# Polynomial convolution and attention on one core: the last quadratic orbit moved onto spare rows by GpSimd transfers

## Chip, core and metric

The kernel runs on one core of one Trainium2 chip. The metric is the time of one execution on the device in microseconds (us); lower is better. Engines are called as the profile calls them: PE (matrix), PEld (its weight loads), DVE (vector), ACT (scalar), POOL (GpSimd) and SP (the queue that issues most transfers).

## What is computed

The input x holds 32 images of 64 channels, 56 x 56 pixels each (N = 3136 pixels). The channels form 8 groups of 8. Two layers follow each other.

```python
# layer 0: polynomial of the 8 channels of a group, per pixel
p2 = x[:, :, _I2] * x[:, :, _J2]                       # 36 products of two
p3 = x[:, :, _I3] * x[:, :, _J3] * x[:, :, _K3]        # 120 products of three
y  = inp + (W2 @ p2 + b2) * beta2 + (W3 @ p3 + b3) * beta3 * 0.1
# layer 1: attention over the 3136 pixels of an image
g = clip(bn(conv1x1(y)), 0, 6)
f = softmax(softmax(theta.T @ theta, axis=1), axis=2)  # theta: first 32 channels of y
out = bn(depthwise3x3(f @ g / h * w)) + y
```

## The kernel before

**Pairs and steps.** The 32 images are worked in 16 pairs. A pair has 49 steps (`IT = 2 * NQ + 1`): a step handles 128 query pixels of one image. In a step PE makes the scores in two halves (`scores`, tile ps), DVE copies each half out of PSUM into the tile e with a running minimum, ACT runs two exponentials over 128 x 3136 values (`first_softmax` and `second_softmax`), and PE multiplies the result of three steps earlier (`LAG = 3`) with g into the accumulators av and ax (`attend`). Into the step's free places go the work of other pairs: convolution steps of a finished pair on DVE (tile y from tt), the matmuls that make g, and the polynomial of the next pair.

**The polynomial.** Its pixels are cut into 13 chunks (`PCS`, 242 pixels, the last one 232). A chunk of a pair has four parts k (two images, two halves of the groups; `ks` is `ALL`); for the first pair's second image only two (`TWO`). A tile of 128 rows is filled by transfers: 32 rows (8 channels of 4 groups) times `NSLOT = 4` slots, interleaved, so that slot s is every fourth row from s. Slot s pairs each channel with the one s further in its group. GpSimd multiplies two such tiles into q (the quadratic orbits 0 to 3) and q with a third tile into p, four times ("0", "2", "4", "b" in `LOADS`; the cubic orbits). PE turns each product into outputs with a 128 x 32 weight from wq, accumulating in `ax[:, AUX:]`. That is five rounds for each k. The sixth round is the last quadratic orbit, channel times channel four further: 32 rows for each k, made in one multiplication for all k (tile p4, from the load xc) and used with its own weight w4. The function `poly` issues the matmuls, `products` the multiplications, `poly_out` the DVE instruction that adds the bias and x and writes y.

**Order.** Every engine runs its instructions in the order in which they are issued (`Pinned`). The order of the products is that of the generator `products`: it goes on in `advance`, called twice a step, as soon as its loads are issued and there is room (`ROOM`: 8 tiles of q, 20 of p). `feed` lists the loads of a chunk, `load_next` issues them on SP, with limits on buffers (`XB`: 7, 13 and 3) and a credit for each half-step. A buffer of a pool is given out again in the order in which it became free.

**Units.** `rounds` in the main loop cuts the six rounds of a chunk into three units of two; a unit stands in a step of its own, so that three units (called U0, U1 and U2 below) take three steps. After some chunks one to three units of g follow, so that the next chunk begins three or four steps after this one. Counted from the loop, the distances between the first units of the 13 chunks in a pair are 4, 4, 3, 4, 3, 3, 3, 4, 3, 3, 4 and 3 steps, and 8 steps from the last chunk to the next pair's first. `split` shares the blocks of `attend` between the two halves of a step by the weight of the units there.

**The start.** The first image is made ahead of the loop in seven slices (`first_loads`, `first_products`, `first_poly`), with DVE doing the products. During the first pair's 49 steps both the rest of pair 0 (13 chunks of two parts) and all of pair 1 (13 chunks of four) are made, so it holds half as much polynomial again as a later pair. The last pair has none.

`_poly_weights` gives each product its weight once: a product that came in an earlier orbit gets zero weight (`if m in seen: continue`). Slot 2's cubic orbit with "0" is channel, channel two further, channel; slot 0 has had it with "2". So the rows of slot 2 in round 1 carry weight zero.

Of the kernel before, what the change touches and what calls it, by code (L numbers as in the profile page):

```python
# [9 lines left out]
FP = mybir.dt.float32  # L10
AF = mybir.ActivationFunctionType
ALU = mybir.AluOpType
# [4 lines left out]
C = G * CPG  # L17
# [18 lines left out]
PCH = -(-N // NPC)  # L36
# [18 lines left out]
]  # L55
NSLOT = 4
NRND = 5
NPROD = sum(1 + len(bs) for _, bs in STEPS)


# [9 lines left out]
def tile_poly_conv_attention(  # L70
# [43 lines left out]
    pe, dve, act, pool, sync = map(Pinned, (nc.tensor, nc.vector, nc.scalar, nc.gpsimd, nc.sync))  # L114

    const = ctx.enter_context(tc.tile_pool(name="const", bufs=1))
    xp = ctx.enter_context(tc.tile_pool(name="xp", bufs=2))
    prp = ctx.enter_context(tc.tile_pool(name="prp", bufs=8))
# [9 lines left out]


    wq = const.tile([128, NRND, 2, 32], FP, name="wq")  # L130
    w4 = const.tile([128, 128], FP, name="w4")
    at = 0
    for s, (_, bs) in enumerate(STEPS):
        for h in range(2) if s < NSLOT else ():
            act.dma_start(
                out=wq[s::NSLOT, :, h, :],
                in_=wpoly[h * 32 : h * 32 + 32, at : at + NRND, h * 32 : h * 32 + 32],
            )
        if s == NSLOT:
            act.dma_start(out=w4, in_=wpoly[:, at, :])  # L140
        at += 1 + len(bs)
    colt = const.tile([128, len(COLS)], FP, name="colt")
    wdt = const.tile([128, 9], FP, name="wdt")
# [12 lines left out]
    for k in range(2):  # L156
        pe.matmul(
            out=ax[:, k * 256 : k * 256 + 256],
            lhsT=w4,
            rhs=wq.rearrange("p k h o -> p (k h o)")[:, :256],  # L160
            start=(k == 0),
            stop=True,
            skip_group_check=True,
        )
# [11 lines left out]
    def row(name):  # L176
        return rowt[:, ROWS.index(name), :]
# [32 lines left out]
    frs = {}  # L210
# [11 lines left out]
    def first_loads(c):  # L222
# [16 lines left out]
        for d in (0, 1):  # L239
# [3 lines left out]
            for k in (0, 1):  # L243
                load(t[k * 32 : k * 32 + 32, :], k, 4 * d, 0, 1)

    def first_products(c):
        xs = fxs[c]

        def product(a, b):
            p = fp[fat["p"] % len(fp)]  # L250
            fat["p"] += 1
            dve.tensor_tensor(p, a, b, ALU.mult)
            return p

        q = {k: product(xs["0", k], xs["a", k]) for k in (0, 1)}
        frs[c] = [q] + [{k: product(q[k], xs[a, k]) for k in (0, 1)} for a in "024b"]
        dve.tensor_tensor(xs["c", 1], xs["c", 0], xs["c", 1], ALU.mult)
        frs[c].append(dict.fromkeys((0, 1), xs["c", 1]))

    first_loads(0)  # L260
    first_loads(1)
# [4 lines left out]
    dve.tensor_scalar(b3row, row("beta3_0"), CONV3_SCALE, None, ALU.mult)  # L266
    for k in range(NRND):
        by = row("beta2_0") if k == 0 else b3row
        w = wq[:, k, :, :].rearrange("p h o -> p (h o)")
        dve.tensor_tensor(w, w, by, ALU.mult)  # L270
    for half in (0, C):
        w = w4[:, half : half + C]
        dve.tensor_tensor(w, w, row("beta2_0"), ALU.mult)
    bias0 = const.tile([128, 1], FP, name="bias0")
    dve.tensor_tensor(bias0, col("b3"), col("beta3_0"), ALU.mult)
    dve.tensor_scalar(bias0, bias0, CONV3_SCALE, None, ALU.mult)
# [80 lines left out]
    def prefetch():  # L357
        while plan and held[plan[0][0]] < XB[plan[0][0]] and credit[0] >= 1:
            load_next()


    ROOM = {"q": 8, "pr": 20}
    taken = dict.fromkeys(ROOM, 0)

    def products(n, c, ks):

        p0, w = PCS[c]  # L370
        ident = f"{n}_{c}_{ks[0]}"

        def use(name, k=None):
            key = n, c, ks, name, k
            return loaded.pop(key)

        x0 = {}
        rounds = [{}]
        both = []
        prods[n, c, ks] = rounds, both  # L380
        yield "q", len(ks)
        for k in ks:
            yield "load", (n, c, ks, "a", k)
            x0[k] = use("0", k)
            xa = use("a", k)
            q = prp.tile([128, PCH], FP, name=f"q_{ident}_{k}", tag="q", bufs=ROOM["q"])[:, :w]
            pool.tensor_tensor(q, x0[k], xa, ALU.mult)
            rounds[0][k] = q
            held["xs"] -= 1
            prefetch()  # L390
        for r, of in enumerate(("0", "2", "4", "b")):
            rounds.append({})
            yield "pr", len(ks)
            for k in ks:
                if of != "0":
                    yield "load", (n, c, ks, of, k)
                xr = x0[k] if of == "0" else use(of, k)
                p = prp.tile([128, PCH], FP, name=f"p_{ident}_{k}_{r}", tag="pr", bufs=ROOM["pr"])[:, :w]
                pool.tensor_tensor(p, rounds[0][k], xr, ALU.mult)
                rounds[-1][k] = p  # L400
                held["x0" if of == "0" else "xs"] -= 1
                prefetch()
        at = slice(ks[0] * 32, ks[-1] * 32 + 32)
        yield "load", (n, c, ks, "c", None)
        yield "pr", 1
        both += use("c")
        p4 = prp.tile([128, PCH], FP, name=f"p4_{ident}", tag="pr", bufs=ROOM["pr"])[at, :w]
        pool.tensor_tensor(p4, both[0], both[1], ALU.mult)
        rounds.append({k: p4 for k in ks})

    feeds = []

    def advance():
# [20 lines left out]
            feeds[0] = gen, None  # L434

    def feed(n, c, ks):
        todo = [("x0" if name == "0" else "xs", name, k) for k in ks for name in "0a"]
        for name in "24bc":
            todo += [("xc", name, None)] if name == "c" else [("xs", name, k) for k in ks]
        for tag, name, k in todo:  # L440
            plan.append((tag, (n, c, ks, name, k)))
        feeds.append((products(n, c, ks), None))
# [12 lines left out]
    def poly(n, c, ks, rs):  # L455

        p0, w = PCS[c]
        rounds = prods[n, c, ks][0]
        at = slice(ks[0] * 32, ks[-1] * 32 + 32)
        for r in rs:  # L460
            for k in ks:
                pe.matmul(
                    out=ax[k * 32 : k * 32 + 32, AUX : AUX + w],
                    lhsT=wq[:, r, k % 2, :] if r < NRND else w4[at, k * 32 : k * 32 + 32],
                    rhs=rounds[r][k],
                    start=False,
                    stop=(r == NRND),
                    skip_group_check=True,
                )
            taken["pr" if r else "q"] -= 1 if r == NRND else len(ks)  # L470

    def poly_out(n, c, ks):

# [276 lines left out]
    def unit(hs, what, todo, out_, blocks):  # L750
        units.append((hs, what, todo, out_))
        weight[hs] = weight.get(hs, 0) + blocks
        if out_ is not None:
            leaves.add(hs)
# [17 lines left out]
            put(hs // 2, f"aux{hs % 2}", go)  # L772

    def poly_unit(n, c, ks, rs, hs):
        ends = rs[-1] == NRND
        unit(
            hs,
            FOR_POLY,
            lambda: poly(n, c, ks, rs),
            (lambda: poly_out(n, c, ks)) if ends else None,  # L780
            1 + 3.6 * len(rs),
        )
        if ends and c == NPC - 1:
            for j in (0, 1):
                if 2 * j in ks:

                    t = hs // 2 + 1 if j == 0 or n == 0 else (n * IT) + 2
                    put(t, "loads", lambda j=j: load_theta(2 * n + j))
# [15 lines left out]

    def first_poly(c):
        p0, w = FCS[c]
        for r in range(NRND + 1):
            for k in (0, 1):
                pe.matmul(
                    out=banks[c][k * 32 : k * 32 + 32, :w],  # L810
                    lhsT=wq[:, r, k, :] if r < NRND else w4[:C, k * 32 : k * 32 + 32],
                    rhs=frs[c][r][k],
                    start=(r == 0),
                    stop=(r == NRND),
                    skip_group_check=True,
                )

# [40 lines left out]
    for n in range(NP):  # L858
# [2 lines left out]
        ga = [("g", n + 1, qs, 0) for qs in GS]  # L861

        def rounds(m, c, ks, per):
            return [("p", m, c, ks, list(range(r, r + per))) for r in range(0, NRND + 1, per)]

        todo = []
        if n == 0:
# [3 lines left out]
            for c in range(NPC):  # L871
                todo += rounds(1, c, ALL, 2)
                if c >= NPC // 2 + 1:
                    k = min(2 if c < NPC - 1 else len(ga), sum(ready(g[2]) <= c for g in ga))
# [3 lines left out]
            at = [2 * base + free[i * (len(free) - 1) // (len(todo) - 1)] for i in range(len(todo))]  # L878
        elif n + 1 == NP:
            todo = gb  # L880
            at = [2 * (base + LAG) + 3 + 4 * i for i in range(len(gb))]
        else:
            at = []
            h = 2
# [38 lines left out]
    for n in range(NP):  # L923
# [11 lines left out]
        for i in range(9 * NB):  # L935
            at = more[i * (len(more) - 1) // (9 * NB - 1)]
# [12 lines left out]
    while t < last + LAG or beside:  # L949
        u = t - LAG  # L950
        new, old = t < last, 0 <= u < last
        todo = []
        if old:
            n, kind, q = tile_at(u)
            todo = [2 * n, 2 * n + 1] if kind == 2 else [2 * n + kind]
# [7 lines left out]
        both = len(todo) == 2  # L963
# [31 lines left out]
def _poly_weights(w2, w3):  # L995
# [4 lines left out]
    at3 = {ijk: k for k, ijk in enumerate(t3)}  # L1000
    wts = np.zeros((2, 2, CPG, 4, NPROD, 2, 2, CPG, 4), np.float32)
    seen = set()
# [18 lines left out]
    assert len(seen) == len(at2) + len(at3)  # L1021
    return wts.reshape(128, NPROD, 128)

# [42 lines left out]
```

## Time and profile before

| | us |
|---|---|
| median of three runs | 4949.45 |
| lowest and highest | 4947.52 and 4963.6 |
| the profiled execution's own time | 4948.12 |
| its span, first to last instruction | 4946.3 |

| engine | busy us | share of the span |
|---|---|---|
| PE | 4734.2 | 96% |
| PEld | 3218.8 | 65% |
| DVE | 4125.5 | 83% |
| ACT | 4554.4 | 92% |
| POOL | 3222.6 | 65% |

The profile is one execution. A group line gives engine, operation, output and inputs, how often, then busy time and mean duration of one instruction, then the engine's idle time ahead of them and what ended it. In a timeline line stand start, duration, engine, operation, how many were merged, and in square brackets the idle time just before with what ended it. All lines are of the helper at line 108, so the names of the tiles tell the instructions apart. Matmuls of one unit run side by side in different columns of the array, so the busy time of a group is what counts and not number times mean.

### The profile page before, as it was taken

To read this page: it belongs to the slowest core of one execution; us is meant where nothing else is said; L and a number is where in the kernel's file an instruction comes from. 1 tells how busy PE (TensorE), PEld (TensorE's weight loads), DVE (VectorE), ACT (ScalarE), POOL (GpSimd) and SP (SyncE) were. 2 spreads that over 40 slices of the span, in tenths; PEclk is the share of its full clock that TensorE was granted. 3 is DMA by queue.
4 is the path that set the end of the run, shared out by engine and by line. 5 is a ranking of instruction groups with operands and counts; after the bars stand their busy time and mean duration, and the time that the engine had idled before them with its cause. 6 is when DMAs were issued, how large, how long until landed. Compare 5 with 4: busy or idle time off the path is not lost.

```text
span 4946.3 us, 264020 instructions
## 1 busy us (share of the span) xinstructions
PE 4734.2 (96%) x118122; PEld 3218.8 (65%) x118122; DVE 4125.5 (83%) x6100; ACT 4554.4 (92%) x2356; POOL 3222.6 (65%) x4335
## 2 busy tenths in 40 slices
PE   6898999999999999999999999999999999999887
PEld 2555666666666666666666666666666666666665
DVE  6545898888888898888889889898888889888887
ACT  1667999999999999999999999999999999999996
POOL 2677685858858586785857768585875858678000
PEclk8999999999999999999999999999999999999999
DMA  7555656565565655556555565656556565654201
GB/s 205 145 152 156 147 144 153 144 152 141 145 141 151 146 145 149 143 143 146 149 143 144 149 143 142 154 144 150 142 145 143 150 144 144 153 142 126 45 11 34
DMA packets 884318, 685.66 MB, mean 139 GB/s; under 512 B 290924, under 2 KB 869356, under 8 KB 879084
## 3 DMA queue, kind: packets, MB, share of 16 engines
q1 hardware_dynamic: 875180, 659.46, 52.5%
q8 instruction: 924, 15.14, 1.3%
q10 hardware_dynamic: 8000, 9.30, 0.6%
q14 instruction: 214, 1.75, 0.1%
HBM read 565.65 MB, written 25.69 MB: 120 GB/s over the span
## 4 chain that ended last, share of the span: by engine, by line
PE 77%; DVE 12%; DMA 3%; issue 3%; ACT 3%; POOL 1%; SPq 1%; ACTq 0%; DVEq 0%; POOLq 0%
PE av L108 33%; PE ps L108 26%; PE ax L108 18%; DVE e L108 10%; ACT e L108 3%; DMA xc_None<-in_x_dram 1%; POOL p L108 1%; DVE y L108 1%; DMA first<-in_x_dram 1%; DVE num L108 1%; DMA x<-in_x_dram 1%; SPq L108 1%; DMA xa<-in_x_dram 0%; DVE rd L108 0%; ACTq L108 0%
## 5 line engine op out<-in xcount | busy, mean ns | idle before, releaser
L108 PEld LDWEIGHTS av<-gq,e 128*64 128x64 f32 x64512 | 2012.2, 138 | 943.9 <-issue 936.2
L108 ACT ACTIVATE e<-e,nm 128x3136 f32<-128x3136 f32 x784 | 2283.6, 2913 | 279.9 <-DVE e L108 264.0
L108 POOL TENSOR_TENSOR p<-q,x 128x242 f32<-128x242 f32 (+1 forms) x2418 | 1824.3, 788 | 815.6 <-PE ax L108 801.2
L108 ACT ACTIVATE e<-e,rz 128x3136 f32<-128x3136 f32 x784 | 2270.3, 2896 | 0.0
L108 PE MATMUL av<-gq,e 128*64 128x65 f32 x64512 | 2225.5, 225 | 3.9 <-ACT e L108 3.1
L108 DVE TENSOR_SCALAR_CACHE_REDUCE e<-ps 128x1568 f32<-128x1568 f32 x784 | 1403.7, 1790 | 314.1 <-PE ps L108 294.2
L108 DVE TENSOR_SCALAR_CACHE_REDUCE e<-ps,nm 128x1568 f32<-128x1568 f32 x784 | 1448.6, 1848 | 255.7 <-PE ps L108 250.1
L108 PE MATMUL ps<-th 32*64 32x392 f32 x25088 | 1449.4, 515 | 120.7 <-DVE e L108 110.7
L108 POOL TENSOR_TENSOR q<-x,xa 128x242 f32<-128x242 f32 x806 | 574.2, 734 | 226.0 <-DMA xa<-in_x_dram 218.0
L108 DVE SCALAR_TENSOR_TENSOR y<-tt,wdt,y 128x605 f32<-128x605 f32 (+6 forms) x711 | 713.1, 1003 | 6.4 <-DMA tt<-tr 5.2
L108 POOL TENSOR_TENSOR p<-q,xb 128x242 f32<-128x242 f32 x806 | 573.9, 739 | 212.3 <-PE ax L108 204.5
L108 PEld LDWEIGHTS ps<-th 32*64 32x64 f32 x25088 | 369.8, 130 | 463.7 <-DVE e L108 381.5
L108 PE MATMUL ax<-gq,e 128*64 128x65 f32 x12288 | 489.7, 222 | 0.7 <-issue 0.6
L108 PE MATMUL ax<-p,wq 128*32 128x242 f32 (+1 forms) x6448 | 481.9, 374 | 1.8 <-POOL p L108 0.2
L108 PEld LDWEIGHTS ax<-gq,e 128*64 128x64 f32 x12288 | 425.0, 138 | 1.0 <-issue 1.0
L108 PEld LDWEIGHTS ax<-p,wq 128*32 128x32 f32 x6448 | 178.4, 109 | 111.8 <-POOL p L108 19.1
L108 POOL TENSOR_SCALAR y<-y,bias 128x616 f32<-128x616 f32 (+2 forms) x79 | 146.9, 1860 | 98.9 <-PE ax L108 98.9
L108 POOL TENSOR_TENSOR p<-xc_None 128x242 f32<-128x242 f32 (+3 forms) x208 | 127.6, 614 | 109.5 <-DMA xc_None<-in_x_dram 91.0
L108 DVE SCALAR_TENSOR_TENSOR y<-ax,bias,xc_None 128x242 f32<-128x242 f32 (+3 forms) x208 | 97.1, 467 | 116.8 <-PE ax L108 116.8
L108 PE MATMUL ax<-wit,y 128*64 128x64 f32 x3136 | 144.2, 223 | 11.7 <-issue 7.5
L108 PE MATMUL ax<-p,w 128*32 128x242 f32 (+1 forms) x1612 | 123.9, 370 | 32.1 <-POOL p L108 32.1
L108 ACT ACTIVATION_READ_ACCUMULATOR e<-e,nm 128x1 f32 x784 | 145.5, 186 | 0.0
(86 smaller groups left out, 1389.4 us busy)
## 6 DMA issues: line engine op xcount, KB each, us to landing
x<-in_x_dram SPq DMA_DIRECT2D x2232, 121.0 KB
xa<-in_x_dram SPq DMA_DIRECT2D x744, 121.0 KB
xb<-in_x_dram SPq DMA_DIRECT2D x1488, 60.5 KB
th<-y SPq DMA_DIRECT2D x124, 392.0 KB
xc_None<-in_x_dram SPq DMA_DIRECT2D x360, 121.0 KB
x<-in_x_dram SPq DMA_DIRECT2D x186, 116.0 KB
out_dram<-y SPq DMA_DIRECT2D x60, 308.0 KB
tt<-tr SPq DMA_DIRECT2D x128, 100.0 KB
```

The costliest lines, as they stand in the source:

```text
L108: i = f(*args, **kw)
```

## The change

The sixth round goes. The 32 rows of a k in p4 are now copied, by a transfer that GpSimd issues, onto the rows of slot 2 in that k's product of round 1, whose own values there are not needed; the weight of the last orbit is added into wq at those rows, where it was zero. So that p4 is there in time it is made first in a chunk, and its load is listed first; so that the transfer has time to land, round 1 is the last round that PE takes: the order of rounds is 0, 2, 3, 4, 1. A chunk of four k then has two units of two rounds and one of a single round (for two k: three rounds and two). The slices of the start do the same, with seven times two transfers.

```diff
+SPARE = (2, 1)
+ORDER = (0, 2, 3, 4, 1)
...
-    w4 = const.tile([128, 128], FP, name="w4")
+    w4 = const.tile([128, 2, 32], FP, name="w4")
+    dve.memset(w4, 0.0)
...
+    def scatter(p, p4):
+
+        pool.dma_start(out=p[SPARE[0] :: NSLOT, :], in_=p4)
...
-        frs[c].append(dict.fromkeys((0, 1), xs["c", 1]))
+        for k in (0, 1):
+            scatter(frs[c][SPARE[1]][k], xs["c", 1][k * 32 : k * 32 + 32, :])
...
+    wr = wq[:, SPARE[1], :, :].rearrange("p h o -> p (h o)")
+    dve.tensor_tensor(wr, wr, w, ALU.add)
...
         prods[n, c, ks] = rounds, both
+        at = slice(ks[0] * 32, ks[-1] * 32 + 32)
+        yield "load", (n, c, ks, "c", None)
+        yield "pr", 1
+        both += use("c")
+        p4 = prp.tile([128, PCH], FP, name=f"p4_{ident}", tag="pr", bufs=ROOM["pr"])[:, :w]
+        pool.tensor_tensor(p4[at, :], both[0], both[1], ALU.mult)
         yield "q", len(ks)
...
                 pool.tensor_tensor(p, rounds[0][k], xr, ALU.mult)
                 rounds[-1][k] = p
+                if r + 1 == SPARE[1]:
+                    scatter(p, p4[k * 32 : k * 32 + 32, :])
...
-        yield "load", (n, c, ks, "c", None)
-        yield "pr", 1
-        both += use("c")
-        p4 = prp.tile([128, PCH], FP, name=f"p4_{ident}", tag="pr", bufs=ROOM["pr"])[at, :w]
-        pool.tensor_tensor(p4, both[0], both[1], ALU.mult)
-        rounds.append({k: p4 for k in ks})
...
-        for name in "24bc":
-            todo += [("xc", name, None)] if name == "c" else [("xs", name, k) for k in ks]
+        todo = [("xc", "c", None)]
+        todo += [("x0" if name == "0" else "xs", name, k) for k in ks for name in "0a"]
+        for name in "24b":
+            todo += [("xs", name, k) for k in ks]
...
-                    lhsT=wq[:, r, k % 2, :] if r < NRND else w4[at, k * 32 : k * 32 + 32],
+                    lhsT=wq[:, r, k % 2, :],
                     rhs=rounds[r][k],
                     start=False,
-                    stop=(r == NRND),
+                    stop=(r == ORDER[-1]),
...
-            return [("p", m, c, ks, list(range(r, r + per))) for r in range(0, NRND + 1, per)]
+            return [("p", m, c, ks, ORDER[r : r + per]) for r in range(0, NRND, per)]
```

In all 806 transfers are issued in the loop, 26 for pair 0 and 52 for each of the 15 other pairs, each of 32 rows of 968 bytes.

## The prediction

> **What bounds the kernel now.** I read the busy table and the chain first, then the steady stretch by itself, since the 49 steps of pair 0 differ from the rest.
>
> ```profile
> PE 4734.2 (96%) x118122; PEld 3218.8 (65%) x118122; DVE 4125.5 (83%) x6100; ACT 4554.4 (92%) x2356; POOL 3222.6 (65%) x4335
> ...
> PE 77%; DVE 12%; DMA 3%; issue 3%; ACT 3%; POOL 1%; SPq 1%; ACTq 0%; DVEq 0%; POOLq 0%
> ...
> L108 PE MATMUL ax<-p,w 128*32 128x242 f32 (+1 forms) x1612 | 123.9, 370 | 32.1 <-POOL p L108 32.1
> ```
>
> They suggest that PE is the bound and that the removed round (`ax<-p,w`, 123.9 us busy and 32.1 us of waiting) is worth up to 156 us. The windows and the waits of 1500 to 3000 us say less:
>
> ```profile
> 1500.00:3000.00 1500.00, 1472.41 (x37747) 1015.38 (x37738) 1310.39 (x1911) 1453.96 (x753) 1069.94 (x1425) 1.00 0.57 146
> ...
> ACT e L108 <- DVE e L108: 40.3, 113, 2.1
> ...
> POOL p L108 <- PE ax L108: 376.8, 125, 28.4
> ```
>
> ACT issues three instructions a step, so 753 are 251 steps of 5.98 us, 293 us a pair. ACT is busy 5.79 us of each and waits 0.16 (40.3 / 251), 7.9 us a pair: that is all a faster PE can win. POOL, busy 71%, waits in that stretch mostly for PE to free its buffers, and no wait of PE for POOL is listed there: POOL is ahead. The timeline shows where ACT waits:
>
> ```profile
> 2031.36 2.92 ACT L108 ACTIVATE e<-e,nm 128x3136 f32<-128x3136 f32 x1
> 2031.42 0.91 PE L108 MATMUL ps<-th 32*64 32x392 f32 x16
> ...
> 2033.58 0.62 PE L108 MATMUL ax<-p,wq 128*32 128x242 f32 x8
> 2034.01 0.59 PE L108 MATMUL ax<-p,w 128*32 128x242 f32 x8
> ...
> 2037.45 2.91 ACT L108 ACTIVATE e<-e,nm 128x3136 f32<-128x3136 f32 x1 [0.29 <-DVE e L108]
> ...
> 2037.62 0.91 PE L108 MATMUL ps<-th 32*64 32x392 f32 x16
> ...
> 2043.42 2.91 ACT L108 ACTIVATE e<-e,nm 128x3136 f32<-128x3136 f32 x1 [0.17 <-DVE e L108]
> ```
>
> This step has U2 and a unit of g; PE needs 6.20 us for it (2031.42 to 2037.62). ACT's starts are 6.09 and 5.97 apart here, against 5.86 where ACT runs without a break. So only 0.23 + 0.11 us are lost around such a step.
>
> **Part 1: the removed round.** In the step shown it takes 0.43 us (2033.58 to 2034.01, one round's distance); PE's 6.20 become 5.77, under 5.86. In the timeline of this pair ten of the 13 chunks show this loss at their last unit, so 10 x 0.34 = 3.4 us a pair, 14 pairs (1 to 14): **-48 us**. In all other steps ACT covers the removal. Bounds: 0 to 7.9 x 14 = 110.
>
> **Part 2: POOL's added work.** POOL's 1069.94 us over 1500 are 16.1 us for each chunk (209 us a pair, 13 chunks, its bias additions `y<-y,bias` included). The change issues four transfers a chunk between the products of round 1. Each waits for its product (POOL's own semaphore), and only then are its descriptors made; the next product stands behind it. No transfer from POOL is in this trace. The nearest row is SP's, and it is of another kind of queue:
>
> ```profile
> 2106.95 0.56 SPq L108 DMA_DIRECT2D x<-in_x_dram  x1
> ...
> 290.86 1.16 SPq L108 DMA_DIRECT2D xc_None<-in_x_dram  x2
> ...
> 296.54 0.61 POOL L108 TENSOR_TENSOR p<-xc_None 128x242 f32<-128x242 f32 x1 [2.46 <-DMA xc_None<-in_x_dram]
> ```
>
> By that row an issue is 0.56 us. The Trainium skill, DMA: Bandwidth & Descriptors, section Specifications, gives about 0.6 us to the first byte for the hardware-made descriptors of SP, which the row agrees with, and about 1 us for GpSimd's, made in software by its own cores. I take 1.0, since the other half of that table fits here, plus 0.1 for the product's semaphore (estimate; bounds 0.65 to 1.6 together). Four make 4.4 us. By the row alone the sum below would have no waits of PE and end 48 us lower than before; by the page it ends above.
>
> A second wait comes with it. Buffers are given out in the order in which they became free. p4 is free after its fourth transfer; three products of round 2 take the three buffers free before it, so the fourth takes p4's own and must wait until all four transfers have landed. Behind it on POOL stand nine products of the chunk, and SP's next loads wait for the buffers that those free. Landing: the xc load above took 4.5 us from the end of its issue to its reader (292.02 to 296.54), for 121 KB from HBM twice over. The skill's same page (Anatomy of one DMA) has about 2.0 us fixed plus bytes / 436e3, an estimate of 2.1 us for 31 KB. Three products cover 2.1 us. So the wait is 0 by the rule and 2.4 by the row; I take **0.8**, as the copy is smaller and not from HBM, but shares DMA engines 57% busy. With 0 the waits of PE below would be 1 to 2 us a pair, with 2.4 some 25.
>
> Together 16.1 + 4.4 + 0.8 = **21.3 us a chunk**. With ACT's 5.86 us a step, a chunk that begins three steps after the last has 17.6 us, one of four steps 23.4. So POOL loses 3.7 in the short ones and regains 2.1 in the long ones. Its reserve: round 2 may not start before PE's U0 of the chunk before (its buffers), and is wanted at the next U0. Of 17.6 us, the unit (1.0), five products (3.8), one transfer and the wait (1.9) use 6.7; for U1 the unit and eight products use 7.2. So about 10.4 us of lateness cost nothing. The distances are 4, 4, 3, 4, 3, 3, 3, 4, 3, 3, 4, 3, 8 steps, and the 8 wipes all lateness out. Lateness: chunk 3 has 3.7, chunk 4 1.6, then 5.3, 9.0, 12.7 (PE waits 2.3, leaving 10.4), 8.3, 12.0 (1.6), 14.1 (3.7), 8.3, 12.0 (1.6). PE waits **9.2 us a pair**, 129 in 14. PE then has no reserve, since ACT is fed step by step. The point from which this decides: with an overrun under 2.7 us a short chunk (transfers plus wait 4.2 us together, 0.86 us a transfer at my 0.8) PE never waits; each 0.1 us above it costs about 1 us a pair.
>
> **Part 3: pair 0.** POOL has no lead there:
>
> ```profile
> 296.54 0.61 POOL L108 TENSOR_TENSOR p<-xc_None 128x242 f32<-128x242 f32 x1 [2.46 <-DMA xc_None<-in_x_dram]
> 297.11 2.03 POOL L108 TENSOR_TENSOR q<-x,xa 128x242 f32<-128x242 f32 x3
> 300.40 7.93 POOL L108 TENSOR_TENSOR p<-q,x 128x242 f32<-128x242 f32 x12
> ...
> 314.62 0.61 POOL L108 TENSOR_TENSOR p<-xc_None 128x242 f32<-128x242 f32 x1 [2.95 <-DMA xc_None<-in_x_dram]
> ```
>
> A chunk takes 18.1 us, of which 14.1 are products and the rest waits for loads that SP issues back to back (26 a chunk at about 0.6). The 5.2 us of transfers and waiting go first into those waits: 14.1 + 5.2 = 19.3 against about 18.5, 0.8 x 13 = 10; the two-part chunks likewise 7.4 + 2.6 = 10.0 against 9.6, 5. If nothing is absorbed it is 13 x 5.2 + 13 x 2.6 = 101. I take **+30**, nearer to the absorbed end.
>
> **Part 4, at nothing.** The seven slices of the start lose a round and wait for 14 transfers; their loads cover it (POOL's first product waits 81 us), at worst 5 us either way. The extra memset and additions on wq are a few DVE instructions. The xc load moves from the end of a chunk's list to its front: in SP's endless order (..., b, xc, 0, a, ...) it keeps its neighbours; it holds its buffer one chunk longer, and with three of them SP could wait a step for `poly_out`, hidden while POOL is ahead by a chunk's loads. The copies add 25 MB to 686. PE's round 1 waits for a transfer issued about a chunk earlier; the cover is gone only if POOL is late, which part 2 counts.
>
> **Sum.** -48 + 129 + 30 = +111 on the profiled execution's 4948.1: 5059; the median of the runs stands 1.3 above it: **5060 us**.
>
> **The rivals.** *POOL's transfers exceed its reserve* (the forecast, 0.67): for it speak 16.1 of 17.6 us already used in short chunks; against it, that no transfer of POOL is in the trace. It runs from 4965 to about 5270 (1.4 us a transfer: overrun 4.9, 22 us a pair, less 3.4, by 14, plus 60).
>
> *The transfers are cheap* (0.28, faster): if one costs POOL under about 0.85 us, as SP's row would have it (4 x 0.65 = 2.6, overrun 1.1), PE never waits for POOL, pair 0 absorbs it, and part 1 remains: 4948 - 48 + 0 to 10, about 4905; down to 4840 if all of ACT's waits went.
>
> *It cancels* (0.05, within 0.3%, which is about what a measurement of this kernel can tell from no change, 15 us): about 0.95 us a transfer, where 5 to 6 us a pair meet the 3.4 and pair 0.
>
> *The full 156 us come off* (under 0.02, inside the second): it would need PE to be the limit in every step; the 5.86 us steps with two whole rounds in them speak against it.
>
> **Numbers.** Faster 0.28, same 0.05, slower 0.67. The range, 4898 to 5270, leaves a tenth at each end.
>
> **What would show it.** Right: POOL busy or waiting on its own transfers for over 20 us a chunk; waits of PE for POOL's p, or for its transfers, in 1500 to 3000 us, at chunks 7 to 12 of each pair; few waits of POOL for PE there; the fourth product of round 2 waiting for a DMA; pair 0 longer. Wrong: ACT's steps at 5.86 without exception and POOL still waiting for PE in each chunk; or a transfer of under 0.8 us between two products.

## The result, and the profile after

| | before | after |
|---|---|---|
| median, us | 4949.88 | 5223.52 |
| lowest and highest | 4947.52 to 4963.6 | 5204.94 to 5239.82 |
| span of the profiled execution | 4946.3 | 5203.2 |

The change made the kernel slower by 5.4%: ratio 1.0543, 95% interval 1.0518 to 1.0568. The forecast was 5060 us: 5223.5 lies inside its range, but the 274 us lost are two and a half times the 111 forecast. The reasons were not those of the forecast, as the trace of after shows. One execution of the 128-partition kernel below (5315.65 us) was in a slower state and is left out of that kernel's median and ratio; with it the median is the 5264 us that a later expectation names.

The page of after: the busy table, the chain by engine, and four groups (busy time, mean ns of one, then the idle time of the engine ahead of them and what ended it).

```profile
PE 4727.0 (91%) x116482; PEld 3195.6 (61%) x116482; DVE 4371.1 (84%) x6101; ACT 4553.9 (88%) x2356; POOL 3575.6 (69%) x5155
...
PE 51%; DVE 25%; issue 10%; DMA 5%; POOL 4%; ACT 2%; SPq 2%; ACTq 0%; POOLq 0%; DVEq 0%
...
L112 ACT ACTIVATE e<-e,nm 128x3136 f32<-128x3136 f32 x784 | 2283.1, 2912 | 529.6 <-DVE e L112 509.0
...
L112 DVE SCALAR_TENSOR_TENSOR y<-tt,wdt,y 128x605 f32<-128x605 f32 (+6 forms) x711 | 980.2, 1379 | 6.4 <-DMA tt<-tr 5.3
...
L112 POOL DMA_DIRECT2D p<-p x806 | 450.8, 559 | 252.9 <-POOL p L112 221.0
```

The same two groups of before, from its page:

```profile
L108 ACT ACTIVATE e<-e,nm 128x3136 f32<-128x3136 f32 x784 | 2283.6, 2913 | 279.9 <-DVE e L108 264.0
...
L108 DVE SCALAR_TENSOR_TENSOR y<-tt,wdt,y 128x605 f32<-128x605 f32 (+6 forms) x711 | 713.1, 1003 | 6.4 <-DMA tt<-tr 5.2
```

PE's share of the chain fell from 77% to 51%, DVE's rose from 12% to 25%. ACT's wait for DVE's e grew by 245 us (264.0 to 509.0). And one group that the change does not touch, the depthwise taps `y<-tt,wdt,y` on DVE (one of the nine products of the 3x3 convolution, added to y; two inputs, tt and y, are in SBUF), took 267 us longer for the same 711 instructions (713.1 to 980.2). POOL's transfer took 0.56 us, and its wait for the product ahead of it 0.3 us (252.9 us over 806).

The steady stretch of 1500 to 3000 us (the line of the windows first, its last three numbers being the granted clock, the DMA share and GB/s; then the waits):

```profile
1500.00:3000.00 1500.00, 1387.27 (x35082) 951.99 (x35082) 1326.09 (x1802) 1368.76 (x709) 1116.15 (x1602) 0.98 0.56 143
...
POOL p L112 <- PE ax L112: 191.7, 37, 28.5
...
ACT e L112 <- DVE e L112: 123.9, 73, 10.3
PE ps L112 <- DVE e L112: 106.4, 104, 9.4
POOL p L112 <- POOL p L112: 70.9, 243, 0.3
POOL p L112 <- DMA p<-p: 37.8, 27, 3.7
```

ACT's 709 instructions are 236 steps where before had 251. Its waits for DVE came to 40.3 us in 113 waits of at most 2.1; now they are 123.9 in 73, the longest 10.3. No wait of PE for POOL is among them. So something stops DVE for some ten microseconds at a time. The view of one tile gives the shortest, middle and longest duration in ns; before and after:

```profile
L108 DVE SCALAR_TENSOR_TENSOR y<-tt,wdt,y x711: 619/953/1471, 554.3 to 4940.8; 128x605 f32<-128x605 f32 x91, 128x616 f32<-128x616 f32 x45, 128x660 f32<-128x660 f32 x14, 128x672 f32<-128x672 f32 x8
```

```profile
L112 DVE SCALAR_TENSOR_TENSOR y<-tt,wdt,y x711: 619/998/12349, 568.0 to 5197.4; 128x605 f32<-128x605 f32 x91, 128x616 f32<-128x616 f32 x45, 128x660 f32<-128x660 f32 x14, 128x672 f32<-128x672 f32 x8
```

The middle hardly moves (953 to 998), but the longest is 12.35 us where it was 1.47. Over 3 us there are 26, before none. One of them in the timeline of after:

```profile
2615.01 0.56 POOL L112 DMA_DIRECT2D p<-p  x1 [0.29 <-POOL p L112]
...
2615.59 5.15 POOL L112 TENSOR_TENSOR p<-q,x 128x232 f32<-128x232 f32 x8
...
2617.14 10.70 DVE L112 SCALAR_TENSOR_TENSOR y<-tt,wdt,y 128x672 f32<-128x672 f32 x1
...
2623.82 2.65 POOL L112 TENSOR_TENSOR q<-x,xa 128x242 f32<-128x242 f32 x4
...
2627.41 0.56 POOL L112 DMA_DIRECT2D p<-p  x1 [0.29 <-POOL p L112]
...
2629.60 1.61 PE L112 MATMUL ps<-th 32*64 32x392 f32 x16 [9.39 <-DVE e L112]
...
2633.21 2.91 ACT L112 ACTIVATE e<-e,nm 128x3136 f32<-128x3136 f32 x1 [10.23 <-DVE e L112]
```

After a chunk's last transfer POOL runs product on product without a gap. A tap starts on DVE at 2617.14 and ends at 2627.84, just after POOL has paused for 0.29 us for its own product (ahead of 2627.41). DVE is in order, so the copies of e stand behind the tap: PE waits 9.39 us for e, ACT 10.23. I call this a hold.

Of the 26 taps over 3 us, 16 end like this one, 0.64 to 0.72 us after POOL's run has stopped for a wait. The other ten end with POOL still busy, each 1.41 us after POOL has begun its bias addition, which has one tensor input where a product has two:

```profile
1525.88 4.92 DVE L112 SCALAR_TENSOR_TENSOR y<-tt,wdt,y 128x605 f32<-128x605 f32 x1
...
1529.40 1.82 POOL L112 TENSOR_SCALAR y<-y,bias 128x616 f32<-128x616 f32 x1
...
1531.20 2.00 POOL L112 TENSOR_TENSOR p<-q,xb 128x242 f32<-128x242 f32 x3
```

In before, taps that start in a gap-free run last 1.08 us on average, against 0.82 when POOL is idle. Its gap-free runs reach 34.7 us, longer than any of after, and none holds a tap. So a long run by itself does not make a hold.

A hold has a second price. PE stands still behind it, and from 2624.7 to 2634.9 the clock granted to PE was half (the third number from the end in the first three lines); the first scores after the hold take 1.61 us (2629.60 above), where later ones take 0.92:

```profile
2614.00:2624.00 10.00, 6.06 (x156) 4.17 (x156) 10.00 (x5) 8.25 (x4) 9.67 (x16) 1.00 0.55 159
2624.70:2634.90 10.20, 5.30 (x88) 3.97 (x94) 7.52 (x8) 1.69 (x1) 5.51 (x9) 0.50 0.56 151
2635.00:2650.00 15.00, 14.18 (x364) 9.63 (x364) 14.20 (x17) 12.37 (x7) 10.91 (x14) 1.00 0.42 111
...
2637.74 0.92 PE L112 MATMUL ps<-th 32*64 32x392 f32 x16
```

From 550 to 5000 us after has 22 stretches at half clock, 154 us in all; 20 of them begin during a hold or within 3 us of its end. Before, from 550 to 4750 us, has none.

Where the time went, from the first e<-e,nm of each pair: 13 us in the start (97.1 to 110.1 us), 1 in pair 0, 241 in pairs 1 to 14 (17 a pair), 2 in pair 15. That is the 257 by which the spans differ.

### The profile page after: what moved, and what is told of

It is laid out like the page before. It is cut to its first block, busy times and chain, and to the rows that moved or that the text cites. A ratio compares the mean times of both kernels' runs of the same rounds, so it can differ in the third digit from the quotient of the medians.

```text
span 5203.2 us, 261265 instructions
## 1 busy us (share of the span) xinstructions
PE 4727.0 (91%) x116482; PEld 3195.6 (61%) x116482; DVE 4371.1 (84%) x6101; ACT 4553.9 (88%) x2356; POOL 3575.6 (69%) x5155
## 4 chain that ended last, share of the span: by engine, by line
PE 51%; DVE 25%; issue 10%; DMA 5%; POOL 4%; ACT 2%; SPq 2%; ACTq 0%; POOLq 0%; DVEq 0%
PE av L112 20%; PE ps L112 20%; DVE e L112 19%; PE ax L112 11%; DVE y L112 5%; POOL p L112 3%; ACT e L112 2%; SPq L112 2%; DMA th<-y 1%; DMA x<-in_x_dram 1%; DMA first<-in_x_dram 1%; POOL q L112 1%; DVE num L112 1%; DMA xa<-in_x_dram 1%; DMA xb<-in_x_dram 1%
## 5 line engine op out<-in xcount | busy, mean ns | idle before, releaser
L112 ACT ACTIVATE e<-e,nm 128x3136 f32<-128x3136 f32 x784 | 2283.1, 2912 | 529.6 <-DVE e L112 509.0
L112 POOL TENSOR_TENSOR p<-q,x 128x242 f32<-128x242 f32 (+1 forms) x2418 | 1728.3, 738 | 661.7 <-PE ax L112 441.1
L112 DVE SCALAR_TENSOR_TENSOR y<-tt,wdt,y 128x605 f32<-128x605 f32 (+6 forms) x711 | 980.2, 1379 | 6.4 <-DMA tt<-tr 5.3
L112 POOL DMA_DIRECT2D p<-p x806 | 450.8, 559 | 252.9 <-POOL p L112 221.0
L112 POOL TENSOR_TENSOR q<-x,xa 128x242 f32<-128x242 f32 x806 | 561.9, 727 | 45.7 <-DMA xa<-in_x_dram 36.5
L112 PE MATMUL ax<-p,wq 128*32 128x242 f32 (+1 forms) x6448 | 508.2, 377 | 34.2 <-POOL p L112 31.4
```

Of the source, the lines that this page charges most:

```text
L112: i = f(*args, **kw)
```

## The experiments

Three theories stood against each other. **1:** gap-free runs of POOL's products behind a transfer hold off DVE's two-input tap until POOL next pauses. **2:** POOL is late for PE (the forecast). **3:** the new order of products and buffers. A *pause* below is two small instructions on POOL, the second of which reads what the first wrote, so that POOL waits on its own semaphore. The last column of the table has the summed time of the taps in the profiled execution and how many lasted over 3 us. In the expectations "round 2" for the transfers' round is the one with index 1.

| kernel | median us | ratio to before, 95% interval | y<-tt,wdt,y us, over 3 us |
|---|---|---|---|
| after | 5223.5 | 1.0543 [1.0518, 1.0568] | 980.2, 26 |
| transfers on SP | 5428.3 | 1.0957 [1.0924, 1.0989] | 852.8, 29 |
| a pause after the transfers | 5003.5 | 1.0104 [1.0077, 1.0130] | 783.6, 10 |
| same instructions, no pause | 5269.2 | 1.0630 [1.0582, 1.0679] | 988.1, 30 |
| before + transfers | 5722.6 | 1.1582 [1.1513, 1.1651] | 1299.0, 98 |
| two pauses | 4989.6 | 1.0082 [1.0069, 1.0095] | 762.4, 3 |
| two pauses, early start | 4981.4 | 1.0059 [1.0048, 1.0071] | 760.4, 2 |
| before, no taps | 4947.6 | 0.9995 [0.9987, 1.0003] | left out |
| after, no taps | 4921.4 | 0.9939 [0.9925, 0.9954] | left out |
| grouped, two pauses, early start | 4921.0 | 0.9946 [0.9933, 0.9960] | 688.6, 0 |
| grouped, no pauses, early start | 5303.4 | 1.0703 [1.0670, 1.0737] | 1015.2, 59 |
| before + 32-partition products | 5597.5 | 1.1303 [1.1270, 1.1337] | 1202.2, 55 |
| before + 128-partition products | 5258.9 | 1.0595 [1.0559, 1.0632] | 966.2, 32 |
| the last with two pauses | 4972.3 | 1.0046 [1.0029, 1.0063] | 751.3, 2 |
| the 32-partition one with two pauses | 4994.1 | 1.0087 [1.0067, 1.0107] | 769.6, 0 |

Before itself: 4949 to 4951 us in these comparisons, taps 713.1 us, none over 3 us.

**Transfers on SP.**

```diff
-                    scatter(p, p4[k * 32 : k * 32 + 32, :])
+                    sync.dma_start(out=p[SPARE[0] :: NSLOT, :], in_=p4[k * 32 : k * 32 + 32, :])
```

> In the loop SP issues the 806 transfers, at the same places, instead of POOL; the start keeps POOL's. Theory 1 (after a transfer of its own POOL keeps the read path[...] through its whole run of products, and DVE's y<-tt, with two inputs in SBUF, stands behind it): y<-tt falls from a mean of 1.38 us back to about 1.0, none over 2 us, and the time goes to 4900 to 4960 us (the 48 us of the removed round won, the 13 us of the start still lost, some loads late on SP). Theory 2 (POOL's added time makes it late for PE): about the same time, since POOL is relieved of the transfers too, but y<-tt keeps its long ones. Theory 3 (the new order of p4, round 1 and the buffers is what costs): no change from 5224.

A miss: 5428 us, slower than after. The waits of the whole run show another cost:

```profile
POOL p L112 <- DMA p<-p: 1291.8, 185, 18.4
...
PEld ax L112 <- POOL p L112: 285.2, 143, 12.2
...
PE ax L112 <- POOL p L112: 218.9, 78, 11.7
```

SP issues a transfer 6.3 us after its product in the middle case, as it takes its list in order; from POOL it was 0.29. POOL then waits for the landing (1292 us, in after 105), because p4's buffer is given out again, and PE waits for POOL: 285 and 219 us, where after has 76 and 31. Here Theory 2's mechanism is real. Besides, 29 taps over 3 us remain without any transfer on POOL, in runs of 21 or 22 instructions, nearly all of which begin after such a wait. So a transfer on POOL is not the only thing that a hold can follow, and this run does not separate the theories.

**A pause after each chunk's last transfer, and its control.**

```diff
                     scatter(p, p4[k * 32 : k * 32 + 32, :])
+                    if k == ks[-1]:
+                        pool.memset(jt[:, 0:1], 0.0)
+                        pool.tensor_tensor(jt[:, 1:2], jt[:, 0:1], jt[:, 0:1], ALU.mult)
```

> As the changed kernel, and after the last transfer of each chunk POOL does two tiny instructions, a memset of one column and a product that reads it and so has to wait for it[...]. It adds about 0.5 us to POOL's chunk. Theory 1 (POOL has to come to a common pause after a transfer before DVE can get in): the long y<-tt go, mean about 1.05 us, time 4910 to 4960. Theory 2 (POOL is late): slower than the changed kernel by up to 2 us a pair times 14, 5225 to 5250. Theory 3 (order): 5224.

The control has the same instructions, but the second reads `jt[:, 2:3]`, which the first does not write, so POOL does not wait.

> The control of the run with the pause: the same two tiny instructions, but the product reads a column that was written once at the start, so that it waits for nothing. Theory 1: no common pause, long y<-tt as in the changed kernel, 5200 to 5240. Theory 2: the same or a little more. If the two instructions alone break the hold, this one is fast as well and the pause is not what matters.

With the pause 5003.5 us, without it 5269.2 (a little above the 5240 expected). The two kernels issue the same number of instructions, transfers and bytes in the same order. The pause alone is worth 266 us, and the taps follow it, 783.6 us against 988.1:

```profile
L112 DVE SCALAR_TENSOR_TENSOR y<-tt,wdt,y x711: 619/911/8970, 569.6 to 4992.6; 128x605 f32<-128x605 f32 x91, 128x616 f32<-128x616 f32 x45, 128x660 f32<-128x660 f32 x14, 128x672 f32<-128x672 f32 x8
```

```profile
L112 DVE SCALAR_TENSOR_TENSOR y<-tt,wdt,y x711: 619/951/12557, 567.5 to 5226.0; 128x605 f32<-128x605 f32 x91, 128x616 f32<-128x616 f32 x45, 128x660 f32<-128x660 f32 x14, 128x672 f32<-128x672 f32 x8
```

Theories 2 and 3 had no room for this: a wait was added to POOL and order and buffers stayed. But 5003.5 is above the 4960 expected, with 10 taps over 3 us left, seven of them in a run that a pause opened: a pause ends a hold but does not rule out the next.

**Before with the transfers added.**

```diff
                 rounds[-1][k] = p
+                if r == 0:
+                    pool.dma_start(out=p[2::NSLOT, :], in_=rounds[0][k][:32, :])
```

It keeps six rounds and writes rows with weight zero.

> The kernel before with all six rounds and its old order, and with the same number of POOL transfers in the loop at the same places (32 rows of q onto the rows of round 1 whose weight is zero). Theory 1: y<-tt gets long as in the changed kernel, time 4949 plus about 280, 5180 to 5280, without the 48 us of the removed round. Theory 2: 5000 to 5250 with waits of PE for POOL. Theory 3 (the order and the single round cost it, not the transfers): 4949 to 4990.

The transfers alone do the harm, more than expected: 5722.6 us, taps 1299.0. Of the 100 taps that began in a run behind a transfer with over 2.2 us of it still to come, 98 lasted over 1.6 us. In the profiled execution, 836 us longer than before's (span 5782.3), the taps take 586 us more. PE's halved clock is part of the rest: 96 stretches and 737 us from 550 to 5450 us, with PE 288 us longer busy on the same matmuls as in before (4734.2):

```profile
PE 5021.8 (87%) x118122; PEld 3393.2 (59%) x118122; DVE 4705.0 (81%) x6100; ACT 4553.8 (79%) x2356; POOL 3521.1 (61%) x5141
```

The two overlap, so they do not add up to the loss. Theory 2 falls here: PE waits 52 us for POOL's products, in before 95. So does Theory 3, as order and buffers are those of before.

**Without taps.** In both kernels `conv_step` returns at once for pairs 0 to 14.

```diff
+        if n + 1 < NP:
+            return
```

> Edit: before, with VectorE's depthwise taps (the instructions y<-tt,wdt,y) of pairs 0 to 14 left out, so that its output lacks them. It is the base for the kernel after with the same left out. VectorE loses some 670 us of work; TensorE and ScalarE keep theirs. All theories: 4850 to 4950 us, since a pair of before takes 293.5 us against 285 us of ScalarE's own work.

> Edit: after, with VectorE's depthwise taps (y<-tt,wdt,y) of pairs 0 to 14 left out, so that its output lacks them. Theory 1 (the loss is those instructions held off by GpSimd): the change no longer costs anything in the loop; what is left is the gain of the removed round, at most 48 us, against 13 us lost in the start: 0 to 40 us under before without taps (ratio 0.992 to 1.000). Theory 2 (GpSimd late for TensorE) and Theory 3 (order and buffers) do not need the taps: still 100 to 270 us over before without taps (ratio 1.02 to 1.055).

Before neither gains nor loses by it (0.9995): its taps were covered. After without taps takes 4921.4 us, 26 less than before without taps. The change now does what its arithmetic says. The groups of e<-e,nm, before and after without taps, and the waits of the latter from 520 to 4350 us:

```profile
L108 ACT ACTIVATE e<-e,nm 128x3136 f32<-128x3136 f32 x784 | 2283.2, 2912 | 280.1 <-DVE e L108 264.5
```

```profile
L112 ACT ACTIVATE e<-e,nm 128x3136 f32<-128x3136 f32 x784 | 2282.7, 2912 | 249.3 <-DVE e L112 218.3
```

```profile
ACT e L112 <- DVE e L112: 60.3, 45, 11.0
...
PEld ax L112 <- POOL p L112: 0.6, 1, 0.6
...
PE ax L112 <- POOL p L112: 0.2, 1, 0.2
```

A pair takes 290.3 us instead of 293.5, 45 us in 14 pairs. PE waits for POOL's products 0.8 us in 13 pairs. Theories 2 and 3 needed 100 to 270 us here and fall.

**A second pause, behind p4.**

> Edit: on top of the kernel with the pause after each chunk's last transfer (5003.5 us), the same two small GpSimd instructions, the second reading what the first wrote, also after each chunk's product of the last orbit (p4). In that kernel 20 of the 40 instructions y<-tt,wdt,y over 1.6 us began behind a gap-free run of products in which p4 stood and no pause since. Theory 1 (a gap-free run of GpSimd products can hold VectorE's two-input y<-tt,wdt,y off until GpSimd next pauses on a semaphore; the run after a transfer nearly always does, the run through p4 sometimes): the long ones become fewer than 15, the sum of y<-tt,wdt,y falls from 784 to about 740 us, time 4950 to 4985 us. Theory 2 (GpSimd is late for TensorE): two more instructions and a wait on GpSimd, 0.6 us a chunk, cost time: over 5010 us. Theory 3 (the new order of products and buffers): unchanged, about 5005 us.

Of the 40 taps over 1.6 us 28 are left, where fewer than 15 were expected, and time and sum are a little above the forecast (4989.6 and 762.4). Only three last over 3 us. The other 25, of 1.6 to 2 us, begin within 0.4 us of the issue of a transfer that has one product behind it, and end some 0.7 us after that product.

**The start made early.** In `first_products` the product of the last orbit comes first, its transfer right behind its target, and its loads are issued first. In this kernel later loads write over the input that `first_out` adds, so that part of the sum is other data.

> Edit: as the kernel with both pauses, and in the start VectorE's product of the last orbit is made first and moved as soon as its target is written, with the other rounds' products behind it (its loads are issued first too). What it tests: the first softmax began at 97.1 us before and at 110.2 us after the change, and the records show TensorE waiting 15.5 us for the transfers of the start to land (4.7, 3.2, 2.5 and 5.0). Theory 1 for the start (the landing of a transfer that GpSimd issues is what TensorE waits for, and work put under it hides it): the first e<-e,nm comes at 98 to 103 us, and the time is 6 to 12 us under that of the kernel with both pauses. If the start's delay is something else (GpSimd's issue, the weights added up): no difference between the two. Against before, Theory 1 for the loop expects 4935 to 4975 us.

As Theory 1 expected for the start, the first e<-e,nm comes at 100.6 us instead of 108.6, and the time is 8.2 us lower. Against before it stays above the 4935 to 4975 expected. I put that down to the short holds just told; the next kernel tests it. PE's waits in the start of after show what it hides:

```profile
54.89 1.92 PE L112 MATMUL first_s<-y,wq 128*32 128x448 f32 x4 [4.71 <-DMA y<-first]
...
67.11 1.41 PE L112 MATMUL first_s<-y,wq 128*32 128x448 f32 x4 [3.24 <-DMA y<-first]
...
78.67 1.90 PE L112 MATMUL first<-y,wq 128*32 128x448 f32 x4 [2.52 <-DMA y<-first]
...
94.84 0.95 PE L112 MATMUL first<-tt,wq 128*32 128x448 f32 x1 [5.03 <-DMA tt<-first]
```

**The transfers in one group.** The start's tiles are now kept as they were, so that nothing is written over. All of a chunk's transfers follow its last product of that round, then one pause; the pause behind p4 stays.

```diff
-                if r + 1 == SPARE[1]:
-                    scatter(p, p4[k * 32 : k * 32 + 32, :])
+                if r + 1 == SPARE[1] and k == ks[-1]:
+                    for kk in ks:
+                        scatter(rounds[-1][kk], p4[kk * 32 : kk * 32 + 32, :])
+                    pool.memset(jt[:, 0:1], 0.0)
+                    pool.tensor_tensor(jt[:, 1:2], jt[:, 0:1], jt[:, 0:1], ALU.mult)
```

> Edit: after, with each chunk's transfers issued one behind the other once the last product of round 2 is written (only the last of them waits for a product), one pause behind them, one pause behind each chunk's p4 as before this run, and the start's moves made early, with their tiles kept as they were. Theory 1 (a run of GpSimd products behind a transfer holds VectorE's y<-tt,wdt,y off until GpSimd next pauses): no product stands directly between two transfers any more, so the 28 instructions of 1.6 us and more that the kernel with both pauses still had go below 10, the sum of y<-tt,wdt,y comes to 715 to 740 us, the first e<-e,nm at 98 to 103 us, and the time to 4915 to 4945 us, under before. Theory 2 (GpSimd late for TensorE): the transfers land later than one by one, so TensorE waits longer for round 2: 4985 us or more. Theory 3 (order and buffers): about as the kernel with both pauses, 4980 to 4990 us.

> Edit: the kernel with grouped transfers and the early moves in the start, without any of the added pauses. Theory 1 (it is the pause that ends the hold, not the grouping): the whole gap-free run behind the four transfers holds y<-tt,wdt,y off, sum 850 to 1050 us, time 5080 to 5250 us. If the grouping alone mends it (the holds come from products that stand between transfers): within 20 us of the kernel with grouping and pauses.

4921.0 us with the pauses: 0.5% under before (ratio 0.9946 [0.9933, 0.9960]), the fastest full kernel of this study. Two taps over 1.6 us are left, and the first e<-e,nm comes at 99.8 us. Without the pauses the same order takes 5303.4 us, slower than after and than the 5250 expected. So the grouping removes the short holds, and the pause is what removes the long ones. The timeline of the fast one:

```profile
2306.72 0.86 DVE L112 SCALAR_TENSOR_TENSOR y<-tt,wdt,y 128x616 f32<-128x616 f32 x1
...
2308.08 2.18 POOL L112 DMA_DIRECT2D p<-p  x4
...
2310.46 0.19 POOL L112 TENSOR_TENSOR jt<-jt 128x1 f32<-128x1 f32 x1
...
2312.58 0.80 DVE L112 SCALAR_TENSOR_TENSOR y<-tt,wdt,y 128x560 f32<-128x560 f32 x1
```

The four transfers take 2.18 us, and the tap behind the pause lasts 0.80 us. Over the whole run:

```profile
L112 DVE SCALAR_TENSOR_TENSOR y<-tt,wdt,y 128x605 f32<-128x605 f32 (+6 forms) x711 | 688.6, 969 | 6.8 <-DMA tt<-tr 5.6
```

**What starts a hold.** No transfer here: before gets one more product behind each product of round 1, into a tile that nothing reads, on 32 partitions or on all 128.

```diff
                 rounds[-1][k] = p
+                if r == 0:
+                    pool.tensor_tensor(ju[:32, :w], rounds[0][k][:32, :], xr[:32, :], ALU.mult)
```

> Edit: before, with one more GpSimd product behind each product of round 1 in pairs 0 to 14, on 32 partitions only, into a tile that nothing reads; no transfer. It asks what starts the hold. Theory 1a (any GpSimd instruction in which only some partitions[...] work puts them out of step and starts a hold): y<-tt,wdt,y has instructions over 2 us and a sum of 850 us or more, time over 5050 us. Theory 1b (only the issue of a transfer does): sum 710 to 750 us, none over 2 us, time 4945 to 4965 us, since GpSimd's load goes from 16.1 to about 18.7 us a chunk, under the 20.3 from which TensorE would wait. Theory 2 (GpSimd's added work by itself makes the loss): as 1b, for the same reason, or up to 30 us more if the two small waits matter.

> Edit: as the kernel with the added products on 32 partitions (5597.5 us, sum of y<-tt,wdt,y 1202 us), but the added product is on all 128 partitions; it takes GpSimd as long (0.70 us). Theory 1a (it is the unequal share of GpSimd's cores that starts a hold): no hold, y<-tt,wdt,y 710 to 770 us with none over 2.5 us, time 4945 to 4985 us. Theory 2a (it is GpSimd's added load and its longer runs without a pause, whatever their partitions): as with 32 partitions, y<-tt,wdt,y over 1000 us, time over 5400 us. Between the two, say 5050 to 5300 us, both would have a part.

5597.5 and 5258.9 us: ordinary products bring the holds as well, and with equal shares too. Neither the transfer nor partitions left out are needed; with 32 partitions there are more holds. So neither theory has it alone: the second time lies in the band where both would have a part. With 128 partitions the timeline shows:

```profile
2264.51 0.83 DVE L108 SCALAR_TENSOR_TENSOR y<-tt,wdt,y 128x605 f32<-128x605 f32 x1
2264.63 2.41 POOL L108 TENSOR_SCALAR y<-y,bias 128x616 f32<-128x616 f32 x1
2267.01 5.36 POOL L108 TENSOR_TENSOR p<-q,x 128x242 f32<-128x242 f32 x8
...
2270.38 12.42 DVE L108 SCALAR_TENSOR_TENSOR y<-tt,wdt,y 128x616 f32<-128x616 f32 x1
```

One tap, beside the bias addition, lasts 0.83 us; the next, beside products, 12.42 us, and ends when POOL next waits, as all 32 here do. The places recur from pair to pair: of the 32 long taps 30 began 12.2 or 15.0 us into their run.

**Pauses in those two kernels,** one behind the last added product of a chunk, one behind p4.

> Edit: the kernel with the added products on all 128 partitions (5264 us), with two pauses a chunk (two small GpSimd instructions, the second reading what the first wrote): one behind the last added product, one behind p4. Theory 1 in its wider form (a long gap-free run of GpSimd instructions can hold y<-tt,wdt,y off, whatever stands in it, and a pause ends that): at most 5 instructions over 3 us where there were 32, sum of y<-tt,wdt,y under 800 us (966 without), time 4950 to 5010 us. If the pause helps only behind a transfer: as without the pauses, 5230 to 5310 us. If the added load is what costs: over 5264 us, since the pauses add 0.6 us or more a chunk to GpSimd.

> Edit: the same two pauses a chunk in the kernel with the added products on 32 partitions (5597 us). Theory 1 in its wider form: the hold ends at the first pause, so what is left are short holds among the added products themselves: sum of y<-tt,wdt,y 750 to 900 us (1202 without), time 4960 to 5120 us. If the pause helps only behind a transfer: about 5600 us.

Both fall back, as expected: 5258.9 to 4972.3 us and 5597.5 to 4994.1. The pause ends a hold whatever started it.

## Why the prediction was wrong

The direction held, the mechanism did not.

- **Part 4, "at nothing", is the step that failed.** It looked at what the change adds to DVE (a memset and some additions) and not at what DVE runs beside POOL. The taps `y<-tt,wdt,y` took 267 us more, and without taps the whole loss turns into a gain of 26 us. None of the rivals named it.
- **Part 2, +129 us of PE waiting for POOL, was about 0.** A transfer cost POOL 0.56 + 0.29 us, not 1.1. The issue was as long as SP's row (0.56), so here the row was right; the Trainium skill's 1 us (DMA: Bandwidth & Descriptors, Specifications) is a time to the first byte and was the wrong quantity. The wait for p4's buffer is there, 37.8 us in some 63 chunks, 0.6 us each, where 0.8 was taken. The chunk came to 19.5 us (1116.15 busy + 70.9 + 37.8, over the 62.7 chunks that 1500 us hold at 311 us and 13 chunks a pair), under the 20.3 at which PE would wait. By the prediction's own threshold this was the case of its second rival, 4905 us, and 4921 without taps came near it, with the start's 13 us on top.
- **Part 1, -48 us, was right:** 45 us in 14 pairs without taps, 39 in the grouped kernel with them, seen only when the holds are gone.
- **Part 3, +30 us for pair 0, was 1 us** (406.0 to 407.0; 7 without taps): POOL's waits for loads, 78 us from 115 to 515 us before, are 17 after, so they took the transfers in.
- **Part 4's start, within 5 us either way, was +13:** the slices' loads cover DVE, but a slice's last product has the transfer behind it, and PE stood 15.5 us for four landings.
- Its range (4898 to 5270) took in 5223.5 by luck, through a term of the wrong kind: 22 us a pair of lateness at a dear transfer, where it was 17 a pair of holds at a cheap one.

What remains open is what starts a hold. The Trainium skill, SBUF — State Buffer, section Who interferes with whom, says that a DVE instruction with two SBUF inputs contends with a GpSimd one that reads SBUF, and calls the port pair that they share an exclusive lock. The taps fit that, but before shows the two sharing at 0.26 us a tap, and the other traces a tap blocked over more than fifteen instructions of POOL; the length of the gap-free run does not tell the two apart. The same skill, GPSIMD Engine Reference, section Instruction dispatch, says that consecutive instructions are no barrier between GpSimd's cores. Cores out of step might never leave the path free together until POOL waits for itself; the pauses, the 32-partition products and the transfers agree with this, the 128-partition products do not ask for it, and the holds that end in a bias addition show that a wait is not the only way out. No run shows the cores, so it stays a reading.

## What to carry to other kernels

Work added to GpSimd has a second price, on VectorE's two-input instructions beside it: look at the longest of them, not at the mean, whenever GpSimd is given more to do. If one lasts as long as GpSimd's remaining run, let GpSimd wait on its own result once or twice a chunk (two tiny instructions), group its transfers in front of such a wait, and measure again with the VectorE work left out to see what the change is worth by itself.

## What the hardware showed that was not expected

- A single DVE instruction of about 1 us lasted up to 12.6 us beside a gap-free run of GpSimd products. It ended when GpSimd next waited (a wait of 0.3 us for its own product was enough) or, in ten cases of 26, during an instruction of GpSimd with one tensor input.
- During or behind such holds the clock granted to TensorE was half for 3 to 14 us at a time in after.
- One pause a chunk (two instructions, 0.12 + 0.19 us) was worth 266 us; two a chunk were worth 287 (5258.9 to 4972.3), 382 (5303.4 to 4921.0) and 603 us (5597.5 to 4994.1).
- A transfer issued by GpSimd occupied it for 0.56 us and, four in a row, 0.54 each; its landing took 2.9 us in the middle case.
